# Router logits of a convolutional expert block: stationary weights and a turned-back result, and output scaling moved two steps ahead

## The chip, the cores and the metric

The kernel runs on one core of a Trainium2 chip. A core has five engines that work side by side, each through a queue of its own, in order: TensorE (PE in the profile, with its weight loads shown as PEld), VectorE (DVE), ScalarE (ACT), GpSimd (POOL) and SyncE (SP), which issues most of the DMAs. [...] The metric is the device time of one execution in microseconds (us), as the median of several runs. The kernel before takes 3235.93 us, the median of three runs that lie between 3234.93 and 3240.06.

## What is computed

The reference is a decoder of four layers with twelve blocks, each followed by a residual sum and a layer norm, over 128 sequences of 64 tokens with 128 features. The change is in the ninth block, `_L2_ffn_ref`, a convolution with a soft mixture of experts:

```python
xc = depthwise causal convolution of x over the sequence (3 taps), + dw_bias
xc = silu(xc @ pw_w.T + pw_b)
x1 = x + xc
logits = x1 @ router_w.T + router_b                  # 8 experts
top_v, top_i = lax.top_k(logits, 2)
rw = one_hot(top_i) weighted by softmax(top_v)
ye = silu(x1 @ expert_w + expert_b)                  # for all 8 experts
moe_out = (sum over experts of rw * ye) @ out_w.T + out_b
h = rmsnorm(x1 + moe_out) * norm_w
ff = gelu(h @ ff_down_w.T + ff_down_b) @ ff_up_w.T + ff_up_b
return h + ff
```

The result is added to the block's input and normalised over its features.

## The kernel before

The 8192 tokens are cut into 16 chunks of 512 tokens, and a chunk into 4 token tiles of 128 (`TPC` = 4). All chunks stay resident as `X[c]`, tokens on the partitions. `ffn_conv` works on pairs of chunks, eight turns in all (`turns`). The work of a pair has three parts:

- `begin(i)`: turn both chunks so that features are on the partitions (`xT_ps`, L1662, copied by ACT to `xp`, L1665); convolution and pointwise product as three accumulating matmuls a chunk (`pw_ps`, L1673), Silu on ACT (L1675), residual sum on POOL (L1676), which gives `x1T`; then `logits` for each chunk (L441 to L450) and `top2` for the pair (L452), a row of small DVE operations on 8 token tiles by 8 experts, with one Tanh on ACT (L462).
- `units(i, n, t)`, one for each of the eight token tiles: two pairs of matmuls for the eight experts (`ye_ps`, L1694, and the bias, L1696), Silu on ACT (L1698), scaling by the router weights on DVE (L1699), and three halving sums on DVE or POOL (L1700) and POOL (L1701, L1702).
- `end(i)`: turn the sums (`sT_ps`, L1709), output projection with the residual (`z`, L1718 and L1719), bias and squares (L1721, L1723, L1724); `norm`, which takes the reciprocal root for this pair's RMS norm and the layer norm of the pair before in one chain on DVE (L340 to L345); scaling by the norm and its weights (L1735, eight operations a pair); turning the scaled output (`oT_ps`, L325, through `transposed`); the biased input and its sum with the output on POOL (L393, L1738); down projection for both chunks (`dn_ps`, L1743), Gelu (L1745), up projection (`u`, L1751) and the last sum (L1753).

The three parts are generators. The loop in `ffn_conv` (L1776 to L1798) emits the eight units of pair i, and behind each of them a step or several of `begin(i + 1)` and `end(i - 1)`, by the list in L1781 to L1797. This gives the program order. The order in an engine's queue is not quite that one: the framework's scheduler places an instruction once its inputs are ready by its own estimate, with the program order as priority. So in the profile the first bias addition of the logits (fifth step) stands in DVE's queue ahead of a reduce of the fourth step.

In `logits` the chunk is the stationary operand: for each token tile its 128x128 block of `x1T` is loaded as weights, and the 8 columns of the router's matrix move through. The result has tokens on the partitions, and DVE adds the bias (L449). `bank` gives the PSUM tiles of this stage from three rotating buffers; `ye_ps` has five of its own. `work(tag, ...)` gives SBUF tiles from small rotating sets.

The kernel has another form of the same product in its sorted mixtures: `gate_rows` and `gate_turned` (L534 to L547) keep the router's 32 padded columns stationary, let 512 tokens move, copy the 32 rows to SBUF and turn them back with transposes. Their rows are in the profile.

## Time and profile before

| | |
|---|---|
| median of the runs | 3235.93 us |
| the profiled execution: time | 3240.21 us |
| its span, first to last instruction | 3238.4 us |
| granted TensorE clock, mean | 0.952 |
| PE matmuls busy | 2889.3 us (89%) |
| PE weight loads busy | 2120.7 us (65%) |
| DVE busy | 1979.3 us (61%) |
| ACT busy | 1638.5 us (51%) |
| POOL busy | 1470.8 us (45%) |
| convolution, first logits to last projection | about 2174 to 2540 us |
| its eight turns, logits to logits | 41.9 to 44.3 us |
| logits matmuls L445 in this stage | 128, 256 ns at the median |
| their bias additions L449 | 16, 192 ns |
| scalings L1735 | 64, 342 ns at the median, 1398 at most |
| expert scaling L1699 | 64, 1219 ns |

Busy time is the sum over an engine's instructions; matmuls are pipelined and their ends are modelled, so successive ones overlap in the records. A fp32 matmul appears as two records, a transpose as one. In the lists by time a line gives the start, the duration, the engine, the line of code and the operation, what it writes and reads with the shape of the tile, and, in brackets, how long the engine stood idle before it and whose result ended that. An `x4` merges four instructions of a kind. The window table gives for each stretch the busy time of each engine with the number of instructions and the clock that was granted to PE.

### The profile page before, as it was taken

The page shows a single profiled execution, that of the slowest core. Times are in us where ns is not written, and L with a number is a line of the kernel's source. Part 1 is how long each engine was busy: PE and PEld are TensorE (multiplying, and loading weights), DVE is VectorE, ACT ScalarE, POOL GpSimd, SP SyncE. Part 2 cuts the span into 40 slices and gives each one's busy share as a digit, 9 for nine tenths or more (in the row PEclk, how much of TensorE's full clock was granted, in tenths as well). Part 3 has the DMA queues.
Part 4 walks back from the last instruction along what each step waited for, and adds up shares of the span by engine and source line. Part 5 has one row for each costly group of instructions (what it writes and reads, how often), then busy time and mean ns, then how long its engine had stood idle before and what let it go on. Part 6 is the DMA issues. An engine that isn't in the chain of part 4 may idle for free. (4 is left out here: it accounts for less than half of the span.)

```text
span 3238.4 us, 110324 instructions
## 1 busy us (share of the span) xinstructions
PE 2889.3 (89%) x47200; PEld 2120.7 (65%) x47200; DVE 1979.3 (61%) x7116; ACT 1638.5 (51%) x3130; POOL 1470.8 (45%) x1500
## 2 busy tenths in 40 slices
PE   5999899988887999999999989998888669997993
PEld 3789866656666777666677767763444337776893
DVE  3732289767776666332366656666778876675245
ACT  3444388745444555333356545643445546654453
POOL 4477554245554444211244445556666223336154
PEclk9999999999998999999999989988998789998997
DMA  5578711000003000000000000000000000001584
GB/s 143 153 210 261 224 52 34 8 2 3 3 3 93 4 4 4 4 1 1 14 4 4 4 5 4 4 12 1 1 1 7 4 1 19 18 13 59 182 263 143
DMA packets 142459, 159.23 MB, mean 49 GB/s; under 512 B 16720, under 2 KB 118096, under 8 KB 141968
## 3 DMA queue, kind: packets, MB, share of 16 engines
q1 hardware_dynamic: 128064, 123.65, 12.8%
q0 software_dynamic: 13184, 27.03, 3.3%
q8 instruction: 370, 6.06, 0.8%
q10 hardware_dynamic: 720, 1.50, 0.2%
q14 instruction: 121, 0.99, 0.1%
HBM read 121.44 MB, written 30.67 MB: 47 GB/s over the span
## 5 line engine op out<-in xcount | busy, mean ns | idle before, releaser
L1201 DVE TENSOR_REDUCE m<-s_ps 128x8 f32<-128x512 f32 x640 | 397.5, 684 | 146.3 <-PE s_ps L1529 50.5
L1250 ACT ACTIVATE e<-t_ps 128x512 f32<-128x512 f32 x640 | 329.9, 601 | 152.9 <-PE t_ps L1243 152.4
L1268 PE MATMUL av_ps<-vx,e 128*64 128x18 f32 (+1 forms) x10240 | 341.1, 216 | 7.3 <-issue 7.3
L1268 PEld LDWEIGHTS av_ps<-vx,e 128*64 128x64 f32 x10240 | 322.5, 140 | 28.1 <-issue 21.5
L1145 POOL TENSOR_SCALAR eb<-qT,small 128x512 f32<-128x512 f32 x80 | 131.5, 1643 | 432.6 <-ACT qT L948 197.6
L774 ACT ACTIVATE hT<-h_ps,aux 128x256 f32<-128x256 f32 x496 | 207.1, 470 | 219.6 <-PE h_ps L772 124.6
L1231 PE MATMUL t_ps<-eb,kT 32*64 32x128 f32 x10240 | 283.4, 287 | 6.6 <-ACT e L1250 2.2
L805 POOL DMA_INDIRECT got<-l_rout,pli x192 | 193.0, 1005 | 178.0 <-issue 64.4
L380 POOL TENSOR_SCALAR x<-xb,lnmv,ln_y 128x128 f32<-128x128 f32 x240 | 188.7, 798 | 173.6 <-DVE ln_y L345 173.6
L772 PE MATMUL h_ps<-ebT,rw 128*128 128x256 f32 x992 | 243.5, 390 | 14.4 <-DVE ebT L760 10.0
L1231 PEld LDWEIGHTS t_ps<-eb,kT 32*64 32x64 f32 x10240 | 200.2, 133 | 72.9 <-DVE m L1201 25.2
L785 PEld LDWEIGHTS yg<-rw,hT 128*128 128x128 f32 x1984 | 241.5, 192 | 6.4
L785 PE MATMUL yg<-rw,hT 128*128 128x128 f32 x1984 | 241.9, 275 | 0.0
L1193 PE MATMUL s_ps<-eb,qT 32*64 32x256 f32 x5120 | 217.4, 399 | 18.2 <-POOL eb L1145 9.6
L380 POOL TENSOR_SCALAR x<-r,lnmv,ln_y 128x128 f32<-128x128 f32 x100 | 79.4, 807 | 293.3 <-DVE ln_y L345 246.9
L786 DVE TENSOR_TENSOR yo<-yg,aux 128x256 f32<-128x256 f32 x124 | 52.5, 424 | 260.8 <-PE yg L785 260.7
L1273 DVE RECIPROCAL rc<-av_ps 128x32 f32<-128x32 f32 (+1 forms) x192 | 61.7, 322 | 244.5 <-PE av_ps L1268 244.1
L772 PEld LDWEIGHTS h_ps<-ebT,rw 128*128 128x128 f32 x992 | 184.1, 196 | 38.3 <-DVE ebT L760 12.6
L747 POOL DMA_INDIRECT aux<-in_x_dram,plt x156 | 158.3, 1015 | 60.4 <-issue 26.1
L1143 ACT ACTIVATE eb<-qT,small 128x512 f32<-128x512 f32 x160 | 106.8, 715 | 128.9 <-POOL qT L1370 123.6
L1145 POOL TENSOR_SCALAR eb<-kT,small 128x512 f32<-128x512 f32 x80 | 145.3, 1816 | 21.8 <-ACT kT L950 10.9
L1193 PEld LDWEIGHTS s_ps<-eb,qT 32*64 32x64 f32 x5120 | 114.4, 134 | 57.1 <-POOL eb L1145 13.4
(437 smaller groups left out, 6446.1 us busy)
## 6 DMA issues: line engine op xcount, KB each, us to landing
rw<-in_l0w_dram SPq DMA_DIRECT2D x78, 512.0 KB
rw<-in_l3w_dram SPq DMA_DIRECT2D x46, 512.0 KB
l_rout<-yo SPq DMA_DIRECT2D x124, 128.0 KB
aux<-xd SPq DMA_DIRECT2D x46, 128.0 KB
aux<-in_l0b_dram SPq DMA_DIRECT2D x78, 66.0 KB
xd<-vx SPq DMA_DIRECT2D x5, 1024.0 KB
x<-in_x_dram SPq DMA_DIRECT2D x16, 256.0 KB
cin<-in_ctx_dram SPq DMA_DIRECT2D x16, 256.0 KB
```

Of the source, the lines that this page charges most:

```text
L380: (V if on_dve else G).tensor_scalar(X[c][:, t, :], r[:, t, :], mv[:, t, 0:1], y[:, t : t + 1], ALU.subtract, ALU.mult)
L747: s.gather = G.indirect_dma_start(out=eb[:, i, :], out_offset=None, in_=x[:, :], in_offset=bass.IndirectOffsetOnAxis(ap=tokens[:, 2 * g + ...
L772: s.pe = mm(ps[:, j * GR : (j + 1) * GR], w1[:, (k + j) * P : (k + j + 1) * P], ebT, start=True, stop=True)
L774: s.act_ins = A.activation(hT[k + j], ps[:, j * GR : (j + 1) * GR], s.act, bias=v[:, k + j : k + j + 1])
L785: s.pe = mm(y[:, i * P : (i + 1) * P], hT[k][:, i * P : (i + 1) * P], w2[:, k, :], start=(k == 0), stop=(k == FK - 1))
L805: s.gather = G.indirect_dma_start(out=got[i][k][:, t, :], out_offset=None, in_=s.rout[b][:, :], in_offset=bass.IndirectOffsetOnAxis(ap=whe ...
L1145: ins = (G if h == 2 else V).tensor_scalar(dst, x, mine, None, ALU.mult)
L1193: mm(ps[g][j * S : (j + 1) * S, u * 256 : (u + 1) * 256].rearrange("p (h k) -> p h k", h=4), rows32(s["q"], g)[:, b], rows32(s["eb"], g)[: ...
L1201: last = V.tensor_reduce(s["m"][:, g, 2 * hf : 2 * hf + 2, :].rearrange("p t h -> p (t h)"), ps[g].rearrange("p (n k) -> p n k", k=S), AX. ...
L1231: mm(ps[g][i * S : (i + 1) * S].rearrange("p (a u j q) -> p a u j q", u=2, a=2, j=2)[:, :, u, j, :], rows32(s["k"], g)[:, b], rows32(s["eb ...
L1250: last = A.activation(e[:, g, :], ps[g], AF.Exp, scale=scale)
L1268: mm(av[j * S : (j + 1) * S, 8 * (u - u0) + n, :], ev[:, n // 2, n % 2, u, j, :], vx[:, 2 * (2 * hf + u) + j, n, :], start=True, stop=True,)
```

## The change

There are three edits. The router's weights are padded from 8 to 32 columns. In `begin`, the two calls of `logits` become one product for the pair with these weights stationary: two matmuls of 32 columns over 512 tokens write rows 0 to 31 and 32 to 63 of one PSUM tile; ACT copies the 64 rows to SBUF (`lgT`); after a step's end four transposes of 64 rows turn them back, and one DVE addition brings in the bias for both chunks, picking the 8 used columns of each 32. `begin` has six steps now instead of seven: the matmuls and the copy are the fifth, and transposes, addition and `top2` the sixth. In `end`, the eight scalings get a step of their own; turning, biased input and sum follow in the next steps. The loop's list takes that step behind unit 4, together with one step of `begin`, where it took two steps of `begin`.

```diff
@@ _COLS
-    ("l2fr", 8, lambda i: i["L2_ffn_router_w"].T),
+    ("l2fr", 32, lambda i: np.pad(i["L2_ffn_router_w"].T, ((0, 0), (0, 24)))),
@@ begin
+            ps = bank("lg_ps")
+            for n in pair:
+                mm(ps[32 * n : 32 * n + 32], col("l2fr"), s["x1T"][n], start=True, stop=True)
+            l = work("tmp", (64, 512), "lgT")
+            A.copy(l, ps[:64])
+            yield
+            ps = bank("lgr_ps")
+            for t in range(TPC):
+                nc.tensor.transpose(ps[:, t * 64 : t * 64 + 64], l[:, t * P : (t + 1) * P], ident[:64, :64])
             R = work("t1", (P, 5, 2 * TPC, E8), "route")
-            for n in pair:
-                logits(s["x1T"][n], col("l2fr"), E8, row("l2frb"), "lg", R[:, 0, n * TPC : (n + 1) * TPC])
-                yield
+            V.tensor_tensor(
+                R[:, 0].rearrange("p (n t) e -> p t n e", n=2), ps[:, : 64 * TPC].rearrange("p (t n e) -> p t n e", t=TPC, n=2)[:, :, :, :E8],
+                row("l2frb")[:, None, None, :].to_broadcast([P, TPC, 2, E8]), ALU.add,
+            )
             s["w"] = top2(R, 2 * TPC)
             yield
@@ end
                 for t in range(TPC):
                     V.scalar_tensor_tensor(h[:, t, :], h[:, t, :], y[:, 0, n, t : t + 1], row("normw"), ALU.mult, ALU.mult)
+            yield
+            for n in pair:
+                h = acc[n]
                 hT.append(transposed(h, "oT"))
                 b = with_bias(2 * i + n, "upb")
                 G.tensor_tensor(b, b, h, ALU.add)
@@ the loop's list
                 elif g == 4:
-                    take(b, 2)
+                    take(e)
+                    take(b)
                 elif g == 5:
                     take(b)
                 elif g == 6:
```

## The prediction, made before the result was known

> **What bounds the kernel now.** I first read the shares on the page: PE is busy for 89% of the span, but every stage has its own limit, so I turned to the stage that is edited. The convolution runs from about 2160 to 2540 us. A turn is one round of its loop over pairs of chunks. I cut the stage at the first logits matmul (L445) of each turn. The window table shows, for each stretch, its length, the busy time of PE, weight loads, DVE, ACT and POOL, then the granted clock:

> ```profile
> 2281.32:2323.17 41.85, 37.04 (x154) 18.57 (x154) 34.05 (x77) 20.66 (x39) 27.39 (x28) 0.96 0.00 1
> 2323.17:2367.11 43.94, 40.22 (x153) 19.78 (x153) 33.72 (x77) 20.55 (x39) 26.92 (x28) 0.88 0.00 0
> 2367.11:2411.24 44.13, 39.80 (x152) 19.46 (x152) 33.53 (x77) 20.54 (x39) 27.34 (x28) 0.88 0.00 1
> ```

> So a steady turn takes 44.1 us, and PE is nearly always busy in it, partly because the clock is only 0.88. I work on the third of these turns. Its chain of waits (start, duration, what) goes back and forth between engines:

> ```profile
> 2365.87 1.19 POOL box L1676
> ...
> 2367.11 1.06 PE lg_ps L445 x8
> 2368.16 0.96 PE ye_ps L1694 x2
> 2369.12 0.79 PE lg_ps L445 x8
> 2370.31 3.49 PE ye_ps L1694 x4
> ...
> 2380.98 1.15 DVE rms_y L345
> 2382.27 0.68 DVE lns L375 x2
> 2384.22 1.33 DVE acc L1735
> ```

> After the logits the chain is DVE's: the reciprocal root of both norms (L340 to L345, called the norm chain below), then the eight scalings L1735. DVE's queue in order of time shows where it loses time:

> ```profile
> 2368.20 0.19 DVE L449 TENSOR_TENSOR route<-lg_ps,rows 128x32 f32<-128x32 f32 x1 [2.46 <-PE lg_ps L445]
> 2368.31 0.68 DVE L1724 TENSOR_REDUCE cv<-sq 128x4 f32<-128x512 f32 x1
> 2369.95 0.19 DVE L449 TENSOR_TENSOR route<-lg_ps,rows 128x32 f32<-128x32 f32 x1 [0.97 <-PE lg_ps L445]
> 2370.06 0.16 DVE L1727 TENSOR_SCALAR cv<-cv 128x8 f32<-128x8 f32 x1
> ```

> Both bias additions of the logits (L449) stand ahead of L1727, the start of the norm chain, and DVE waits 2.46 + 0.97 = 3.43 us in front of them. PE's queue in order of time shows who waits for the scalings:

> ```profile
> 2370.24 3.56 PE L1694 MATMUL ye_ps<-w_l2f,box 128*128 128x512 f32 x4
> 2374.05 1.98 PE L1694 MATMUL ye_ps<-w_l2f,box 128*128 128x512 f32 x4
> 2378.52 1.98 PE L1694 MATMUL ye_ps<-w_l2f,box 128*128 128x512 f32 x4
> 2383.67 0.95 PE L325 MATMUL oT_ps<-ident,acc 128*128 128x128 f32 x2 [3.17 <-DVE acc L1735]
> ```

> PE stands 3.17 us before the first turning of the scaled output (oT). The four expert matmul records of 1.98 us took 3.56 right behind the logits: half clock.

> **The logits, part by part.** *PE.* Removed: 16 records of L445 in two lots, start to start 2368.02 - 2367.11 = 0.91 and 2369.85 - 2368.96 = 0.89, together 1.80. Added: two matmuls 32 columns wide over 512. The same form is the down projection L1743, whose four records take 1.72 in the chain of waits, 0.43 each. [...] L1743 is just such a pair and does not overlap, so I take 1.72. The four transposes of 64 rows take 0.22 to 0.27 us each in the early router (L546) but are pipelined; four turnings of a chunk (L1662) take 0.66 with the tail, 0.43 start to start. I take 0.43. PE: +1.72 + 0.43 - 1.80 = +0.35. PE's wait of 3.17 at oT covers it; uncovered it is 6 x 0.35 = 2.

> *ACT.* One copy, 0.58 by L540 (32 rows; the time goes with the 512 elements of a row). ACT is busy 20.5 of 44 and idle for 2.54 ahead of 2370.40, just there. Uncovered: 6 x 0.58 = 3.5.

> *DVE.* Two additions of 0.19 become one of 128x64, 0.22 by L526 (a copy of that size). Gain 0.16 at most. The weight is in the queue. The new addition needs both halves of the pair, then a copy, then four transposes. It is ready later, and DVE's order, made from estimated readiness, should place it behind L1727. The chain can then start when the second reduce L1724 can: its squares (ACT) end at 2366.89, the reduce takes 0.6 to the next start, so L1727 at about 2367.70 instead of 2370.06: 2.36 earlier.

> *The clock.* Half clock followed the logits in six of the seven turns, for one or two stretches of 3.4 us, each costing 1.71 of matmul time. [...] But what is it worth? PE waits at oT anyway, so only the units (a unit is one token tile through the eight experts) that feed DVE count: the one whose scaling by router weight (L1699) starts at 2375.41 came 1.2 later than at full clock (3.56 - 1.98 = 1.58, less 0.4 for the transposes in front). So if L1699 of these units keeps its place in the chain, the gain at the end of the chain is 1.2; if the norm chain runs ahead of them, 2.36.

> *Once only.* In the first turn's preparation nothing covers the longer path. Copy 0.58 plus transposes 0.43 less DVE's own lateness there (L449 at 2178.51, 1.4 after its matmuls) gives 0 to 1; I take +1. The table of columns grows by 24, 12 KB on a load of 81.5 KB issued at 1.24 us; PE's first use is at 9.86, behind x and ACT's copy: nothing, 0.2 if uncovered.

> **The scalings.** The same eight operations; no DMA and nothing for SP or POOL moves with them, since turning, copy, biased input (L393) and sum (L1738) keep step 6. In the old order 14 routing operations of top2 lie between the start of the norm chain and the last L1735 (2388.4). Thirteen cost about 0.14 start to start and one 1.2 (L463, beside POOL's sum): 3.1 together. Moved ahead, the eight run in one row: 4.40 and 3.20 for all eight where nothing of top2 lies between (around 2506 and 2532), against 5.4 here. So the last scaling comes 1.2 to 2.4 plus 3.1 earlier, 4.3 to 5.5 in all. Behind them in DVE's queue wait top2 (needed only by the next turn's units, 6.2 us after its end at 2391.2) and L1699 of the last two units.

> **What is late next.** The last unit's sum. The turning of the sums (sT, L1709) starts at 2398.34 and needs POOL's last L1702, which ended at 2398.97: PE arrived just in time. Between 2370.4 and 2399 DVE and POOL take turns: L1735 is 0.33 to 1.40, L1702 0.45 alone and 1.41 beside L1699. Moving eight operations makes none of this work less, so from the 4.3 to 5.5 only the earlier start, 1.2 to 2.4, surely reaches sT; the rest only if top2's tail falls behind the last two units. I take 2.4 per turn: the earlier start in full, or its lower end with part of the tail. Turns 1 to 6 have both logits and scalings: 6 x 2.4 = 14.4. Turn 0 has no end to hasten, turn 7 no logits: 0. With +1 of the preparation: **-13.4**. The profiled execution took 3240.21 (span 3238.4 and 1.8 around it), so 3226.8; it lies 4.28 above the median of the runs, 3235.93, against which the forecast is **3222.5**.

> **The rivals.**
> 1. *Everything reaches sT.* top2's tail falls behind the last units and the 4.9 (mid of 4.3 to 5.5) pass through: 6 x 4.9 - 1 = 28, 3207. PE's floor allows it: 44.1 less 4.3 waits less 5.1 clock plus 0.35 is 35.1 a turn. Against it: top2 stands before those units in program order. 10%.
> 2. *Hidden anyway.* DVE and POOL fill the time as before and the two clock drops merely shift: 0 to -3 in all, 3235. For it: the turn from 2281 with no drop behind the logits is shorter by only 2.2 while its DVE waits are the same. 16%.
> 3. *Slower: the turned logits become the new wait.* If the new addition still stands ahead of L1727, it comes at 2367.11 + 0.86 + 0.94 (expert pair between) + 0.86 + 0.1 + 0.58 + 0.1 + 0.5 = 2371.0, and L1727 at 2371.3, 1.3 late. PE's transposes, queued behind the second matmul, wait 0.8 for the copy, and the experts behind them with it, plus 0.43: 1.2. Together 2.5 x 6 + 1 = +16, 3252. It decides from the point where both the addition precedes the norm chain and the transposes directly follow the matmuls. For it: the old order was just as wrong about readiness (3.43 of waiting). 27%.
> 4. The forecast: 47%.

> That the change does not do what it says is not likely: the early router already works so (L539 to L546).

> **The numbers.** About 0.2%, 6.5 us, can be told from no change. Faster: forecast and rival 1, 57%. Same: rival 2, 16%. Slower: 27%. The range reaches from rival 1's better part (3203, with 5.5 a turn) to rival 3 at 3252. The forecast's own range is 3212 (2.4 plus half of the tail and a covered preparation) to 3230 (1.2 a turn).

> **What would show it.** Right: turns of about 41.7 between the first logits matmuls; DVE's L1727 about 0.8 behind the second square, ahead of the routing addition; no 3 us of DVE waiting for logits; clock 1.0 behind the logits; eight L1735 in one row; oT's wait on PE under 2; and a new wait of sT for L1702. Wrong: DVE or PE waiting over 1 us around the lgT copy with L1727 behind it (rival 3), or turns of 44 with sT waiting for all that oT gained (rival 2).

## The result, and the profile after

| | before | after |
|---|---|---|
| median of six runs each, side by side | 3236.39 us (3232.9 to 3242.63) | 3223.4 us (3220.2 to 3229.8) |
| ratio, 95% interval | | 0.9955 [0.9941, 0.9969] |
| profiled execution: time, span | 3240.21, 3238.4 us | 3222.37, 3220.6 us |
| stage: first pointwise matmul to last down projection | 369.1 us | 359.6 us |
| of it six turns, second to eighth lot of logits | 260.6 us | 253.8 us |
| half-clock loss in these six turns | 29.0 us | 17.1 us |
| PE idle in these six turns | 27.1 us | 26.7 us |

The kernel is 13.0 us faster by the medians; 3222.5 was forecast. "Half-clock loss" is the time missing to full clock, one minus the granted clock, summed over the stretch; one interval of 3.41 us at half clock loses 1.71. The two profiled executions lie 17.8 us apart, but 7.6 of this is ahead of the stage, where the engines' order is unchanged: over the traces of this study the stage begins anywhere between 2159 and 2180 us. So I compare the stage and its turns, which repeat well (before, in two traces: 369.1 and 368.9; after, in three: 359.6, 359.8 and 357.9). The eight lots of logits bound seven stretches. The first, 21.3 us in before, covers only the preparation and the front of the first turn; the 41.9 to 44.3 us given above for the turns hold for the other six.

The window table of after, cut at the first logits matmul (now L1681) of two successive turns, has the columns of the table shown of before:

```profile
2356.03:2398.31 42.28, 37.42 (x145) 16.97 (x145) 34.68 (x77) 21.00 (x40) 26.48 (x28) 0.96 0.00 1
2398.31:2440.67 42.36, 38.92 (x145) 17.04 (x145) 34.68 (x77) 20.99 (x40) 26.55 (x29) 0.92 0.00 1
```

A turn takes 42.3 us instead of 44; the clock went from 0.88 to 0.92 or 0.96. DVE, ACT and POOL are about as busy as before. DVE's queue in order of time, in the first of these turns:

```profile
2356.57 0.74 DVE L1738 TENSOR_SCALAR cv<-cv 128x8 f32<-128x8 f32 x1
...
2360.19 0.23 DVE L1689 TENSOR_TENSOR route<-lgr_ps,rows 128x64 f32<-128x64 f32 x1 [1.45 <-PE lgr_ps L1687]
...
2367.93 4.94 DVE L1746 SCALAR_TENSOR_TENSOR acc<-acc,rms_y,rows 128x128 f32<-128x128 f32 x8
```

The norm chain starts (L1738, before L1727) 0.54 behind the logits instead of 2.95, and the 3.43 us of waiting ahead of it are gone. The one addition that is left (L1689) waits 1.45 in the middle of the chain. The eight scalings (L1746, before L1735) run in one row and end at lg+16.8 (16.8 us behind the first logits matmul) instead of lg+21.4. PE's queue in the same turn:

```profile
2356.03 1.04 PE L1681 MATMUL lg_ps<-box,cols 128*32 128x512 f32 x2 [0.72 <-POOL box L1676]
2357.34 1.05 PE L1681 MATMUL lg_ps<-box,cols 128*32 128x512 f32 x2 [0.26 <-POOL box L1676]
...
2359.69 0.46 PE L1687 MATMUL lgr_ps<-ident,lgT 64*128 64x64 f32 x4
2360.08 1.98 PE L1705 MATMUL ye_ps<-w_l2f,box 128*128 128x512 f32 x4
...
2368.33 0.33 PE L325 MATMUL oT_ps<-ident,acc 128*128 128x128 f32 x1 [1.80 <-DVE acc L1746]
2369.06 0.33 PE L325 MATMUL oT_ps<-ident,acc 128*128 128x128 f32 x1 [0.40 <-DVE acc L1746]
2369.59 0.33 PE L325 MATMUL oT_ps<-ident,acc 128*128 128x128 f32 x1 [0.20 <-DVE acc L1746]
...
2371.39 0.48 PE L325 MATMUL oT_ps<-ident,acc 128*128 128x128 f32 x1 [0.47 <-DVE acc L1746]
...
2375.21 1.05 PE L1757 MATMUL dn_ps<-oT,cols 128*32 128x512 f32 x4
...
2379.78 1.16 PE L1765 MATMUL u<-w_l2f,g 32*128 32x128 f32 x16 [0.96 <-ACT g L1759]
...
2383.02 1.09 PE L1720 MATMUL sT_ps<-ident,box 128*128 128x128 f32 x8
```

Behind the logits the expert matmuls take 1.98 again, full clock, where the turn shown of before had 3.56. PE still waits for the scalings, but in pieces of 1.80, 0.40, 0.20 and 0.47 instead of 3.17 and 0.45. The turning of the sums (sT) has no wait for POOL. New is a wait of 0.96 for the Gelu ahead of the up projection `u`.

Why did 4.6 us at the scalings become 1.8 a turn, and by which way? The groups of lines, each over its kernel's six turns (count | busy us, mean ns | idle in front), compare the same 194 expert records. First before, then after:

```profile
L1694 PE MATMUL ye_ps<-w_l2f,box 128*128 128x512 f32 x194 | 114.7, 707 | 0.0
```

```profile
L1705 PE MATMUL ye_ps<-w_l2f,box 128*128 128x512 f32 x194 | 106.9, 662 | 0.2 <-ACT units L1709 0.2
```

The same work costs PE 7.8 us less, and the six turns are 6.8 shorter, at equal idle time. That pointed to the clock, which my forecast had priced low.

### The profile page after: what moved, and what is told of

Same layout as the page of the kernel before. It is cut to its first block, busy times and chain, and to the rows that moved or that the text cites. A ratio compares the mean times of both kernels' runs of the same rounds, so it can differ in the third digit from the quotient of the medians.

```text
span 3220.6 us, 110214 instructions
## 1 busy us (share of the span) xinstructions
PE 2877.4 (89%) x47136; PEld 2097.9 (65%) x47136; DVE 1987.4 (62%) x7108; ACT 1640.6 (51%) x3138; POOL 1466.2 (46%) x1500
## 5 line engine op out<-in xcount | busy, mean ns | idle before, releaser
L772 PE MATMUL h_ps<-ebT,rw 128*128 128x256 f32 x992 | 241.9, 388 | 13.4 <-DVE ebT L760 9.3
L1231 PEld LDWEIGHTS t_ps<-eb,kT 32*64 32x64 f32 x10240 | 198.2, 132 | 73.3 <-DVE m L1201 25.3
```

The lines of the kernel that those rows point to most:

```text
L772: s.pe = mm(ps[:, j * GR : (j + 1) * GR], w1[:, (k + j) * P : (k + j + 1) * P], ebT, start=True, stop=True)
L1231: mm(ps[g][i * S : (i + 1) * S].rearrange("p (a u j q) -> p a u j q", u=2, a=2, j=2)[:, :, u, j, :], rows32(s["k"], g)[:, b], rows32(s["eb ...
```

## The experiments

Two theories stood against each other. **Chain:** the turn is as long as the way from the logits over norm chain and scalings to oT and sT; the gain is what this way got shorter. **Clock:** PE's idle time in a turn is given by the other engines and hardly moves; the gain is half-clock time that no longer occurs.

All runs in one table; ratios are to the kernel before in the same comparison, the other columns from the profile, in us. The last column is read in the steady turns. (The expectations of e_logits and e_scale count the stage up to the last record of the down projection, some 1.6 us more than the table: 370.7 before and 361.2 after.)

| run | ratio [95%] | stage | six turns | half-clock loss | PE idle | last scaling, lg+ |
|---|---|---|---|---|---|---|
| before (before2) | | 369.1 (368.9) | 260.6 (260.3) | 29.0 (29.0) | 27.1 (27.0) | 21.4 |
| after | 0.9955 [0.9941, 0.9969] | 359.6 | 253.8 | 17.1 | 26.7 | 16.8 |
| after2 | 0.9964 [0.995, 0.9978] | 359.8 | 253.9 | 17.1 | 26.8 | |
| after3 | 0.996 [0.9944, 0.9976] | 357.9 | 251.4 | 15.4 | 26.0 | 16.8 |
| e_logits | 0.9947 [0.9932, 0.9961] | 353.1 | 247.3 | 6.8 | 27.7 | 18.0 |
| logits2 | 0.9943 [0.993, 0.9956] | 355.9 | 250.1 | 12.0 | 27.2 | |
| logits3 | 0.9949 [0.993, 0.9969] | 355.9 | 250.2 | 11.9 | 27.3 | 18.0 |
| e_scale | 1.0002 [0.9991, 1.0013] | 370.6 | 261.5 | 32.4 | 26.7 | 20.1 to 21.8 |
| e_scale1 | 0.9952 [0.9933, 0.997] | 355.7 | 248.3 | 10.2 | 26.4 | 18.0 |
| e_late | 0.9966 [0.9953, 0.9979] | 364.6 | 257.8 | 23.9 | 25.3 | 16.3 |
| e_dense | 0.9977 [0.9968, 0.9986] | 369.8 | 262.4 | 18.8 | 27.7 | 19.2 |
| e_nobias | single run | 356.0 | 258.5 | 22.6 | 48.4 | |
| e_nopool | single run | 346.4 | 243.2 | 12.0 | 20.7 | 15.3 |

**e_logits: the logits alone.** The changed kernel with the scalings back in one step with turning and sum, and the list as before.

```diff
-            yield
-            for n in pair:
-                h = acc[n]
                 hT.append(transposed(h, "oT"))
@@ the loop's list
                 elif g == 4:
-                    take(e)
                     take(b)
```

> Only the new logits; the scalings stay in one step with the turning, as before. My theory, that both edits shorten the same DVE chain (norm chain and scalings): about half of the change's gain, 4 to 8 us below the kernel before (3228 to 3232), the stage from first pointwise matmul to last down projection 364 to 367 us (before 370.7, after the change 361.2); L1738's place in the chain moves to 0.6 us behind the first logits matmul, as after the change. Rival, the clock alone: with no 8-column matmuls left no half-clock stretch follows the logits, and the full gain of 13 us is here.

Measured: 3223.68 beside 3242.32 us. The whole gain is there, without the moved scalings. The last scaling comes 1.2 *later* than in the changed kernel (lg+18.0), and the six turns are 6.5 *shorter*. The window table of one of its turns:

```profile
2318.33:2359.61 41.28, 36.57 (x144) 16.53 (x144) 34.41 (x77) 21.33 (x40) 27.61 (x28) 1.00 0.00 1
```

A turn of 41.3 at full clock. The same 194 records of expert matmuls, in its groups of lines:

```profile
L1705 PE MATMUL ye_ps<-w_l2f,box 128*128 128x512 f32 x194 | 100.2, 628 | 0.0
```

Against the chain theory: beside the changed kernel, a longer way to oT and a shorter turn.

**e_scale: the scalings alone.** The kernel before with the step of its own for the scalings, taken behind unit 4 ahead of two steps of `begin`.

```diff
+            yield
+            for n in pair:
+                h = acc[n]
                 hT.append(transposed(h, "oT"))
@@ the loop's list
                 elif g == 4:
+                    take(e)
                     take(b, 2)
```

> Only the scalings moved ahead; logits as before. My theory: the other half, 3 to 8 us below before (3228 to 3233), stage 363 to 368 us; DVE still waits 3.4 us a turn for the logits, half clock still follows them. Rival, the clock alone: no gain, 3234 to 3238, stage 370 to 372.

Measured: no change (3241.98 beside 3242.32), as the clock theory had it. DVE's queue tells why the way to oT hardly got shorter:

```profile
2368.65 0.19 DVE L449 TENSOR_TENSOR route<-lg_ps,rows 128x32 f32<-128x32 f32 x1 [0.97 <-PE lg_ps L445]
2368.76 0.16 DVE L1727 TENSOR_SCALAR cv<-cv 128x8 f32<-128x8 f32 x1
...
2380.96 4.96 DVE L1735 SCALAR_TENSOR_TENSOR acc<-acc,rms_y,rows 128x128 f32<-128x128 f32 x8
```

The chain still starts behind both logits additions, and although the eight run in one row (4.96), they start 15.2 behind the logits and end at lg+20.1 here, in other turns at lg+21.8: 21.4 before. Routing operations that no longer lie between them lie in front of them.

**e_dense: the clock alone.** The kernel before, with one wide matmul ahead of the 8-column matmuls of each chunk; its result is overwritten by them.

```diff
-                logits(s["x1T"][n], col("l2fr"), E8, row("l2frb"), "lg", R[:, 0, n * TPC : (n + 1) * TPC])
+                ps = bank("lg_ps")
+                mm(ps, w[1][:, 0, :], s["x1T"][n], start=True, stop=True)
+                for t in range(TPC):
+                    mm(ps[:, t * E8 : (t + 1) * E8], s["x1T"][n][:, t * P : (t + 1) * P], col("l2fr"), start=True, stop=True)
+                V.tensor_tensor(R[:, 0, n * TPC : (n + 1) * TPC], ps[:, : TPC * E8].rearrange("p (t e) -> p t e", t=TPC), row("l2frb")[:, None, :].to_broadcast([P, TPC, E8]), ALU.add)
```

> The kernel before, with one more 128x128 by 512 matmul in front of each chunk's 8-column matmuls, into the same PSUM tile that they then overwrite: 3.4 us of full-clock TensorE work more in each of eight pairs (two matmuls of two records, 0.86 each, 1.72 a pair). It asks what lowers the clock. If the narrow matmuls do, half clock behind the logits goes in most turns though work is added. Time: if the clock is what the change gained, 0 to 8 us below before; if the clock behind the logits is hidden by the wait for the scalings, as I predicted, 5 to 14 us above before, since the bias additions and the norm chain behind them come 0.86 to 1.72 later in each turn.

Measured: 3235.62 beside 3242.32 us, with more work on PE: two matmuls a turn of two records of 0.43 us, 10.3 us in six turns. PE's queue, and the window behind the first logits (its last columns are clock, DMA share and GB/s):

```profile
2370.44 1.12 PE L1681 MATMUL lg_ps<-box,w_l2f 128*128 128x512 f32 x2 [0.72 <-POOL box L1676]
2371.40 0.95 PE L1683 MATMUL lg_ps<-cols,box 128*128 128x8 f32 x8
2372.21 1.10 PE L1681 MATMUL lg_ps<-box,w_l2f 128*128 128x512 f32 x2
2373.15 0.95 PE L1683 MATMUL lg_ps<-cols,box 128*128 128x8 f32 x8
...
2375.32 1.98 PE L1698 MATMUL ye_ps<-w_l2f,box 128*128 128x512 f32 x4
```

```profile
2370.44:2374.00 3.56, 3.56 (x21) 2.60 (x21) 2.07 (x6) 0.76 (x2) 1.35 (x3) 1.00 0.00 0
```

All 8-column matmuls are still there, and the half clock behind them is gone, here and in five more of seven turns; the experts take 1.98. (The exception is the lot at 2196.61, where PE also waits 1.43 in the interval and the streamed share defined below is 0.27.) So it was what PE streams, not the form of the logits as such. The six turns grew by only 1.8 for 10.3 of added work at nearly the same idle time, while the half-clock loss fell by 10.2. At the price of a microsecond of loss worked out below (0.59) that pays for 6.0 of the missing 8.5; the other 2.5 are unexplained. (The whole time is 6.7 below before while the stage of the profiled execution is level with it. The stages of the other executions are not known, and I have no cause for the difference.)

**e_late: the turned logits one step later.** The changed kernel with transposes, addition and `top2` taken behind unit 6 instead of behind unit 5, to take DVE's 1.45 us wait out of the norm chain.

```diff
-                elif g == 5:
-                    take(b)
                 elif g == 6:
                     take(e, 2)
+                    take(b)
```

> The changed kernel with transposes, bias addition and top2 one step later, behind the turning of unit 6. It takes the routing addition, for which DVE still waits 1.45 us in the middle of the norm chain in each turn, out of that chain. If the chain sets the turn: 1.0 to 1.5 us a turn less, 6 to 9 us below the changed kernel (3214 to 3217). If TensorE's work sets it, so that what the chain gains comes back behind the pointwise matmuls: 0 to 3 below (3220 to 3224). If top2 ends too late for the next turn's first unit: above the changed kernel.

Measured: 3230.89, not better than the changed kernel by its ratio. The wait is gone, and the last scaling comes at lg+16.3, earliest of all complete kernels. But its turns last up to 45.2. The window of one of 44.5:

```profile
2363.13:2407.61 44.48, 40.05 (x145) 18.59 (x145) 35.20 (x77) 21.31 (x40) 25.09 (x28) 0.88 0.00 1
```

Clock 0.88, a loss of 23.9 in six turns. The shortest chain has long turns and a low clock. A late `top2`, the expectation's other reason for a longer time, does not show as waiting of PE: its idle time, 25.3, is the lowest of all complete kernels.

**before2, after2, logits2: the kernels again,** unchanged, and e_logits once more, to see whether the turns and the loss repeat.

> The kernel before once more, for a second profile of its stage. Half clock behind the logits in at least five of seven turns again, if the narrow matmuls cause it; turns of 43.5 to 44.5 us with two half-clock stretches or three, and less than 42.5 only where one is missing.

> The changed kernel once more, on the same chip as the next runs. If the scalings are worth nothing, as the run of the scalings alone says, its time lies within 3 us of the new logits alone; if the half-clock stretches fall by chance of phase, its steady turns (42.3 to 43.6 us before) now vary with the number of such stretches in them, by up to 1.7 us for each, at the same order of work.

> The new logits alone once more, for a direct comparison with the changed kernel. If the first profile of it (turns of 41.3 us, no half clock in four of them) was a lucky phase: some turns now have half clock at the turning of the scaled output and take 42 to 44 us, and the time is that of the changed kernel within 3 us. If moving the scalings costs something: 4 to 8 us below the changed kernel.

Measured: before2 as a single run 3243.94, after2 3235.47, logits2 3230.3, beside 3247.54. The turns of before and after came back within 0.3 us each. Those of e_logits did not in full: the same program lost 6.8 once and 12.0 the second time, and its six turns took 247.3 and 250.1. One program and two loop times, moving with the loss. By the medians logits2 is 5.2 below after2, within the 4 to 8 expected if moving the scalings costs something; the intervals of the two ratios overlap a little.

**e_nobias: less work for PE.** The changed kernel without the experts' bias matmuls; so the experts' bias is missing from the output.

```diff
-                mm(ps[k].rearrange("p (e d) -> p e d", e=4), s["x1T"][n][:, t * P : (t + 1) * P], w[0][:, 4 * k : 4 * k + 4, :], start=True, stop=False, skip_group_check=True)
-            for k in range(2):
-                mm(ps[k], rows32(ones, k), rows32(be, k)[:, k * 512 : (k + 1) * 512], start=False, stop=True, skip_group_check=True)
+                mm(ps[k].rearrange("p (e d) -> p e d", e=4), s["x1T"][n][:, t * P : (t + 1) * P], w[0][:, 4 * k : 4 * k + 4, :], start=True, stop=True, skip_group_check=True)
```

> The changed kernel without the experts' bias matmuls (L1707, 16 a turn, 0.22 us each start to start at full clock), so the output lacks the expert bias. It takes 3.5 us of TensorE's work from each turn and nothing from the DVE chain. If TensorE's work plus its waits set the turn: 2.5 to 3.5 us a turn less, stage 340 us or less (after the change 359.6), time about 3200. If the DVE chain and POOL's sums set it: under 1 us a turn, time 3217 to 3223.

Measured: 3231.89 as a single run, beside 3247.54. This run is inconclusive. PE's idle time rose from 26.7 to 48.4, the turns last anywhere from 38.3 to 45.9 us, and the norm chain starts 2.2 us behind the logits, in one turn 40: the queues were ordered afresh, so it doesn't tell what PE's work is worth.

**e_scale1: the scalings one step ahead instead of two.** The changed kernel with the step of the scalings taken behind `top2`'s step (behind unit 5).

```diff
                 elif g == 4:
-                    take(e)
                     take(b)
                 elif g == 5:
                     take(b)
+                    take(e)
```

> The changed kernel with the scalings one step ahead of the turning instead of two, and behind the transposes, bias addition and top2 of the same step. If the scalings two steps ahead cost their 4 to 6 us because they push top2, and with it the Tanh in ACT's queue and the Gelu behind it, back: as the new logits alone, ratio to before 0.994 to 0.995, loop 247 to 250 us (changed kernel 253.8), no wait of the up projection for the Gelu. If any step of its own for the scalings costs them: as the changed kernel, 0.996, loop 253 to 255.

Measured: 3229.67 beside 3245.6. It behaves like e_logits: last scaling at lg+18.0, six turns 248.3, loss 10.2.

**e_nopool: DVE and POOL relieved.** The changed kernel without the second halving sum (L1712); so the expert sums in the output are not complete.

```diff
-            G.tensor_tensor(y[:, :2], y[:, :2], y[:, 2:4], ALU.add)
```

> The changed kernel without the units' second halving sum on POOL (L1712, 8 a turn, 0.72 each alone), so six of eight experts' shares are partly left out of the output. It takes 5.8 us of POOL's work from each turn. If the sharing of DVE and POOL sets the turn, as a part of my prediction says (what DVE and POOL have to do before the sums are turned): 3 to 6 us a turn less, loop 215 to 235. If TensorE's work, its waits and its half clock make up the turn: the waits for the scalings shrink by the 1 to 2 us of contention in the row of eight, half clock goes with them, loop 240 to 248 us.

Measured: 3219.85 as a single run, beside 3245.6. Of DVE's groups over six turns the scalings shrink, from a mean of 660 to 592 ns, as POOL's share of the work goes. The six turns took 243.2, in the range expected if PE's work, waits and half clock make up the turn, and above the 215 to 235 of the other theory. It is the one run that lowers PE's idle time, to 20.7, mostly in one turn of 33.4. Its steady turn at full clock, 40.8, is only 0.5 shorter than that of e_logits, 41.3, which does all its sums. So POOL's second halving sum costs PE 6.0 us of idle time in six turns; that it is not what holds a steady turn is likely from this one run.

**after3 and logits3: is the second edit worth having?** Both kernels again in one comparison, with more rounds.

> The changed kernel again, beside logits3 in one comparison, to settle whether the part of the change that moves the scalings costs anything. Clock theory (the scalings in one row leave PE waiting four times at oT, and a half-clock stretch follows in nearly every turn): 0.9955 to 0.9965 of the kernel before, and 3 to 6 us above logits3, with about 17 us of half-clock loss between the first and the last logits. Chain theory (scalings two steps ahead shorten the path to oT, the rest is chance): at or below logits3, 0.994 or less.

> The changed kernel with the scalings back in one step with the turning. Clock theory: 0.994 to 0.9955 of the kernel before, 3 to 6 us below after3, half-clock loss of 7 to 12 us between the first and the last logits. Chain theory: at or above after3; no version with the scalings late is faster than the changed kernel.

Measured: 3226.05 and 3224.37 beside 3239.25. In the three comparisons of each the logits alone came to 0.9947, 0.9943 and 0.9949, the whole change to 0.9955, 0.9964 and 0.996; in the stage the logits alone are 2 to 6.7 us ahead. In the last comparison the medians are 1.7 apart, less than expected, and the intervals overlap. So a lead of 2 to 5 us for the version with the scalings left where they were is likely, and not proven by the whole time. That both beat the kernel before is: all six intervals end below 1.

## Why: what went ahead of half clock

The records give the granted clock as stretches of time. In the ten traces of complete kernels examined for this (all but before2 and after2), all changes of the clock in the 3.2 ms, 62 to 76 in each, lie on one regular grid of 3.4133 us, none more than 2 ns off it. So each stretch of half clock lasts one such interval or several. What goes ahead of a drop had to be found from the runs. I worked out, for each interval at full clock, how much PE *streamed* in it, a measure of my own: for every matmul record 0.43 us if it moves 512 fp32 columns (the expert matmuls start 0.43 us apart at full clock), in proportion if fewer (half as much for bf16: the 204-column matmuls of L672 start 0.087 us apart, which makes 0.22 for 512), times the share of the 128 rows that it uses, over 3.41. For the six turns (start of interval, PE busy share by records, streamed share, what the next interval got; those up to 0.36):

```text
before                              after
2192.54 0.33 0.02 half  (wait)      2186.99 0.27 0.22 half  (wait)
2213.02 0.26 0.19 half  (oT)        2238.19 0.53 0.17 half  (oT)
2236.91 0.79 0.28 half  (logits)    2282.57 0.62 0.22 half  (oT)
2250.57 0.20 0.11 half  (oT)        2323.53 0.38 0.12 half  (oT)
2291.53 0.08 0.03 half  (oT)        2333.77 0.64 0.36 half  (u, xT)
2322.25 0.79 0.29 half  (logits)    2367.90 0.58 0.19 half  (oT)
2339.31 0.47 0.15 half  (oT)        2408.86 0.31 0.10 half  (oT)
2366.62 0.86 0.31 half  (logits)
2380.27 0.07 0.02 half  (oT)
2410.99 0.93 0.34 half  (logits)
2424.65 0.06 0.03 half  (oT)
```

(One more of before, the logits at 2455.37 with 0.95 busy, dropped at 0.37.) Over the 655 full-clock intervals in the six turns of ten traces, 64 of them followed by half clock, a bound at a streamed share of 0.37 puts all but 5 on the right side; the best bound on the busy share misses 29. (The 127 of them in before and after, 19 followed by half clock, are all on the right side: the highest share with a drop is 0.37, the lowest without 0.40.) The bound was fitted to these ten; in the four other traces (before2, after2, e_nobias, e_nopool) it puts 1 of 255 full-clock intervals on the wrong side, the bound on the busy share 12. In e_dense the interval with the logits has 0.50 instead of 0.31, and no drop. That experiment moved the share and kept the narrow matmuls, and the clock followed. (The transposes are counted like other matmuls. Left out of the share, 21 intervals instead of 5 are on the wrong side.)

Now each result reads off. In the five intervals of the old logits in the table and below it PE is 79 to 95% busy in the records, but the streamed share is 0.28 to 0.37, as a record of 8 columns starts 0.11 us after the one before and counts 0.007; half clock followed each time. Behind the new logits of after it came only in the first of the six turns, where PE waits 3.47 us between the two halves of the pair. Five of the seven drops of after follow the wait at oT, and there the second edit can do harm: with the scalings in one row PE has turnings, waits of 0.4 and 0.2 and the 32-row bias matmuls side by side. Two windows of after, the second holding the stretch of half clock:

```profile
2366.60:2371.00 4.40, 1.99 (x7) 0.80 (x7) 4.40 (x13) 3.03 (x8) 2.90 (x4) 1.00 0.00 2
2371.00:2374.50 3.50, 3.11 (x6) 1.55 (x7) 3.46 (x7) 1.09 (x3) 2.94 (x3) 0.54 0.00 0
```

In e_logits the same waiting comes in two pieces, with expert matmuls between:

```profile
2372.51 0.33 PE L325 MATMUL oT_ps<-ident,acc 128*128 128x128 f32 x1 [2.40 <-DVE acc L1746]
...
2373.82 1.02 PE L1705 MATMUL ye_ps<-w_l2f,box 128*128 128x512 f32 x2
...
2376.84 0.33 PE L325 MATMUL oT_ps<-ident,acc 128*128 128x128 f32 x1 [1.14 <-DVE acc L1746]
```

Its intervals there hold 0.37 to 0.47, at or just above the bound; those of after 0.10 to 0.22. In the turn of e_late shown above two intervals fall below it, 0.18 at oT and 0.33 behind it. e_logits and logits2 are one program and lost 6.8 and 12.0 us; a turn is not a whole number of intervals (41.28 us is 12.1), so the grid cuts the same work at other places from turn to turn. That this makes the difference between the two is my estimate and was not shown.

How much is a microsecond of loss worth? A straight line through the eleven traces of complete kernels without added work gives six turns = 243.1 + 0.59 x loss, all within 0.8 us. PE's idle time in them is 25.3 to 27.7, whatever the way to oT was. Why the price is 0.59 and not 1 is not shown.

## Why the prediction was right, point by point

The time and the sign were right, and so were most of the single steps. The path by which these steps were to shorten the turn was not: the gain came through the clock, which the forecast priced low, and not through the earlier turning of the sums.

- **Norm chain 2.36 earlier, ahead of the routing addition: right.** 2.41 (lg+0.54 against 2.95). Rival 3 needed the addition ahead of the chain; that didn't happen.
- **Last scaling 4.3 to 5.5 earlier: right,** 4.6. But how it came about was wrong: I gave 3.1 of it to the scalings' move. Alone the move gives between 1.3 and -0.4 (e_scale), behind the new logits 1.2; e_logits has 3.4 of the 4.6. In one row the eight also got slower, from a mean of 582 to 660 ns each over the six turns.
- **PE +0.35: nearly right.** Over six turns the logits records went from 13.2 to 13.4 us busy, and the transposes take 0.39 a turn to the next start: together +0.4 a turn. The copy of 64 rows took 0.58, as forecast from one of 32. But the row that the 1.72 came from was misread as a pair that does not overlap: the two matmuls of the old L1743 started 0.75 us apart, the second only 0.05 us after the end of the copy (L332) that feeds it. In after the down projection's pair (L1757) starts 7 ns apart, and its four records take 1.05 together, shown above: with both inputs ready the two ran at the same time. The logits' pair is not ready together: the second waits for POOL's sum (0.26, 1.30 us behind the first).
- **Clock 1.0 behind the logits: right** in all but the first of the six turns (at 2190.41, within PE's wait of 3.47 us). No long wait went with the old logits' drop: in the interval at 2366.62 the largest gap was 0.72, and in e_dense, with 0.50 streamed in the logits' interval instead of 0.31, full clock followed. One of the six drops that I had counted behind the logits, at 2195.95, followed a wait ahead of them instead (first row of the table above).
- **The clock's worth: the step that failed,** "PE waits at oT anyway, so only the units (a unit is one token tile through the eight experts) that feed DVE count", 1.2. PE's waiting is not a store that full clock would only enlarge: idle stayed at 26.7, and 11.9 us of loss went with 6.8 us of the six turns, 0.57 each. I looked at one turn's wait instead of comparing turns of different clock.
- **What reaches sT, 2.4 per turn: the term of the sum that was too large.** The six turns gained 6.8, 1.1 each, not 14.4, and that gain fits the clock alone (0.59 x 11.9 = 7.0). The earlier oT was partly given back behind the pointwise matmuls: from the first of them to the next logits it was 12.0 and is 14.2, because one unit's experts (four records fewer between the logits and the down projection: 22, now 18) moved there. The new wait of sT for POOL did not come; that wait of PE fell from 3.8 to 1.0 in six turns.
- **Turn 0 nothing, turn 7 nothing, preparation +1: wrong.** The first of the six turns went from 42.7 to 40.0, and behind the last logits lie another 2.2 of gain, and 0.5 ahead of the six turns.
- **Why the total fits all the same:** stage -9.5 (in after3 -11.2) where -13.4 was forecast; the medians show -13.0, with an interval of -10 to -19. The forecast is in the right place by luck: 14.4 was put down to sT, where the clock gave some 7 and the ends of the stage 2.7; the rest of the medians' 13.0 is not traced.

Left open: why the idle time of the six turns stays near 26 us whatever is moved. The traces show where it went. From before to after PE's waits over six turns fell from 16.5 to 13.4 us at oT and from 3.8 to 1.0 at sT, and rose from 6.0 to 9.1 in front of the logits (for POOL's residual sum) and from 0 to 2.9 in front of the up projection (for the Gelu). So 5.9 saved on the chain came back as 6.0 elsewhere. e_logits has no wait for the Gelu and 17.0 at oT. e_nopool (20.7 instead of 26.7) shows that DVE and POOL own a part; the rest was not tried apart.

## What to carry to other kernels

Where a window table shows a granted clock below 1, look at what PE streamed in the interval just ahead of the drop, not at whether it was busy: here intervals with matmuls of 8 columns (79 to 95% busy, streamed share 0.28 to 0.37) and intervals with small pieces between the waits at oT (31 to 62% busy, 0.10 to 0.22) were both followed by half clock. Price a drop by comparing turns of the same loop at different clocks, and don't call it hidden because PE waits later: here 11.9 us of loss went with 6.8 us of the six turns. When two edits come together, measure each alone: here one carried the whole gain, and the other, sound on its own path, probably gave part of it back through the clock.
